# The main branch's last two tiles in an order written out by hand: last weights turned first, last statistics in front of the narrowing

## The chip, the cores and the metric

The kernel runs on one core of a Trainium2 chip. The time is what the device takes for one execution, in microseconds; the kernel before is given as the median of three runs. A core has five engines with an instruction stream each: TensorE (PE) for matrix products, VectorE (DVE), ScalarE (ACT), GpSimd (POOL) and SyncE (SP), which here issues the transfers. An engine takes its instructions in order, so an instruction that waits holds up everything behind it on its engine. TensorE writes its results to PSUM banks, from which DVE and ACT read them.

## The reference, cut to what matters

Two layers, each of which adds an attention branch multiplied by a gate branch to a stream `x` of 2 x 2048 rows of 256 numbers, in float32. The change lies in the second layer's main branch, and in its last step:

```python
x = x + ob @ w_out + b_out                                    # ob: the attention's sums
h2 = _ln(x, ln2_g, ln2_b)                                     # statistics, then scaling
m = gelu(h2 @ w1 + b1, approximate=False) @ w2 + b2           # 256 -> 1024 -> 256
s = x + m                                                     # the main branch's result
...
x = x_in + s * g                                              # g: the gate branch, x_in: the stream
```

The attention is local: a block of 64 queries sees its own and the preceding block of 64 keys, for 16 heads.

## The kernel before, in words

The 4096 rows are 32 tiles (`NT`) of 128 rows, in 8 groups (`NG`) of 4 (`GT`). The gate branch has been computed by the time of interest and lies in `G` (the profile calls its tile `stream`). The main branch is in `main_branch`. `head(g)` prepares a group's queries and keys. `attention(g)` goes over its four tiles. For tile n it has two half tiles, 2n and 2n + 1: `turn_weights` transposes the softmax weights of a half tile (8 transposes of 128x128, L1640), `small` computes the scores of the half tile two further on (`score`, L1607) and then `total`, the weighted sums of this one (L165). The four steps of `finish(n)` end a tile: `take` copies the sums out of PSUM, `divide` transposes them and divides (PE L188, DVE L192), `back` transposes back (PE L252, copy on ACT L254), and `out` multiplies with the output weights and adds the residual on DVE (PE L261, DVE L1672), which gives the tile's row of `y`. `take` stands in the tile's own slot; `divide`, `back` and `out` of tile n - 1 stand in the slot of tile n, so those of the last tile, 31, are left over for `finale`.

`forward(g, t0, nt)` is the feed-forward part of `nt` tiles of a group:

- `moments(t)`: two DVE statistics operations (L79, L80) on a tile of `y`; `ln_rsqrt`: two POOL operations (L84, L85) that give the scale.
- `norm(t)`: DVE scales the tile into `h2` (L88; the profile's `h`), then POOL adds the bias row `b2` to `y` (L1717).
- `turn(c)`: PE transposes `h2`, one half of its columns for each c (L1724), and `affine` copies it to `h2T`, on DVE for c = 0 (L1591) and on ACT for c = 1 (L1589).
- `widen`: four calls of two chunks each; a chunk is two products of 128 hidden units (PE L1741) and a GELU on ACT (L1748). `u` and `ge` hold the result.
- `again(t)`: SP loads the residual rows of a tile again (L1732, into `xs_b`).
- `narrow(t)`: eight products (PE L1754), a DVE sum with `y` (L1758), POOL's product with `G` (L1759) and sum with the residual (L1760), and the output transfer on SP (L1761).

All instructions are recorded in program order; what runs on an engine when follows from that order and the waits. The order comes from `in_turn`: every lane is a list of (weight, step) with a start and an end, each step gets the place of its weight's middle, and the steps of all lanes are sorted by place. A step `none` only takes room. In the last group, `attention(7)` shares its room with the feed-forward part of group 6 (`forward(NG - 2)`) and then with that of the first two tiles of group 7, 28 and 29 (`forward(NG - 1, 0, 2)`, called the pair below). `finale` follows: tile 31's divide, back and out spread over the first 0.6 of the feed-forward of tile 30, and then, alone, the feed-forward of tile 31.

Of the kernel before, what the change touches and what calls it, by code (L numbers as in the profile page):

```python
# [9 lines left out]
ALU = mybir.AluOpType  # L10
# [4 lines left out]
NT = B * S // P  # L15
TPB = S // P
GT = 4
GW = GT * P
NG = NT // GT
# [11 lines left out]
def kernel(ctx: ExitStack, tc: tile.TileContext, io: dict, col: dict):  # L31
    nc = tc.nc
# [57 lines left out]
    def in_turn(*lanes):  # L90

        order = []
        for i, (a, b, lane) in enumerate(lanes):
            total, at = sum(w for w, _ in lane), 0.0
            for w, do in lane:
                order.append((a + (b - a) * (at + w / 2) / total, i, len(order), do))
                at += w
        for _, _, _, do in sorted(order, key=lambda x: x[:3]):
            do()
# [187 lines left out]
    G = stream.rearrange("p (n d) -> p n d", d=D)  # L287
# [531 lines left out]
    with ExitStack() as l0_ctx:  # L819
# [349 lines left out]
        groups, values, zss, accs, scores, turns, outs, ends = {}, {}, {}, {}, {}, {}, {}, {}  # L1169
# [296 lines left out]
        for g in range(NG):  # L1466
            lanes = [(0, 1, attention(g))]
# [12 lines left out]
            if g == NG - 1:  # L1480
                first, second = first_tiles
# [15 lines left out]
    def main_branch(open_pc):  # L1497
# [20 lines left out]
        groups, values, zss, accs, scores, turns, outs, ends = {}, {}, {}, {}, {}, {}, {}, {}  # L1518
# [159 lines left out]
        def attention(g):  # L1678

            lane = []  # L1680
            none = lambda: None
            for n in range(GT * g, GT * (g + 1)):
                divide, back, out = ends[n - 1] if n else [none] * 3
                take, *ends[n] = finish(n)
                ahead = (lambda n=n: project_values(n + 1)) if n + 1 < NT else none

                def small(i):

                    if i + 2 < 2 * NT:
                        score(i + 2)  # L1690
                    total(i)

                first, second = (lambda i=i: turn_weights(i) for i in (2 * n, 2 * n + 1))
                lane += [(1, first), (1.2, none), (0.7, divide), (0.6, none)]
                lane += [(1.2, lambda n=n: small(2 * n)), (1.8, none), (0.5, back), (1, none)]
                lane += [(1, second), (2, none)]
                lane += [(1.2, lambda n=n: small(2 * n + 1)), (0.3, take), (0.8, none), (0.5, out), (0.8, none), (1, ahead), (0.6, none)]
            return lane

        def forward(g, t0=0, nt=GT):  # L1700

            d = {}
            ts = range(t0, t0 + nt)
            w = nt * P

            def moments(t):
                if t == t0:
                    d["mv"] = sb(pc, [P, GT, 2], "f_mv")
                    d["rs"] = sb(pc, [P, GT], "f_rs")
                ln_moments(pc, d["mv"], t, [groups[g]["y"][:, t, :]])  # L1710

            def norm(t):
                if t == t0:
                    d["h2"] = sb(pc, [P, GT, D], "h2", 1)
                y = groups[g]["y"][:, t, :]
                normalize(d["h2"][:, t, :], y, d["mv"], d["rs"], t)
                nc.gpsimd.tensor_tensor(y, y, b2, ALU.add)  # L1717

            def turn(c):
                if not c:  # L1720
                    d["h2T"] = sb(pe, [P, 2, GW], "h2T", 1)
                tp = bank("tp")
                for i, t in enumerate(ts):
                    nc.tensor.transpose(tp[:, i * P : (i + 1) * P], d["h2"][:, t, c * P : (c + 1) * P], ident)  # L1724
                affine(d["h2T"][:, c, 0:w], tp[:, 0:w], c, "c_ln2_g", "c_ln2_b")

            def again(t):

                if (t - t0) % 2 == 0:
                    d["rr"] = sb(pe, [P, GT, P], "xs_b", 2).rearrange("p (a b) n -> p a (b n)", a=2)  # L1730
                d["r", t] = d["rr"][:, (t - t0) % 2, :]
                nc.sync.dma_start(d["r", t], rows_r[:, g * GT + t, :])  # L1732

            def widen(cs):
                if not cs[0]:
                    u = sb(pe, [P, HC, GW], "u", 1)
                    d["m"] = [u[:, c, :] for c in range(HC)] + [sb(pe, [P, GW], "ge") for _ in range(8 - HC)]
                for c in cs:
                    mm = bank("s")[:, 0:w]
                    for k in range(2):  # L1740
                        nc.tensor.matmul(  # L1741
                            mm,
                            lhsT=cw["w1"][:, k, c * P : (c + 1) * P],
                            rhs=d["h2T"][:, k, 0:w],
                            start=(k == 0),
                            stop=(k == 1),
                        )
                    nc.scalar.activation(d["m"][c][:, 0:w], mm, AF.Gelu, bias=cc("c_b1", c))  # L1748

            def narrow(t):  # L1750
                mm = bank("s")[:, 0:D]
                i = t - t0
                for c in range(8):
                    nc.tensor.matmul(  # L1754
                        mm, lhsT=d["m"][c][:, i * P : (i + 1) * P], rhs=cw["w2"][:, c, :], start=(c == 0), stop=(c == 7)
                    )
                out = groups[g]["y"][:, t, :]
                nc.vector.tensor_tensor(out, mm, out, ALU.add)  # L1758
                nc.gpsimd.tensor_tensor(out, out, G[:, g * GT + t, :], ALU.mult)  # L1759
                nc.gpsimd.tensor_tensor(out, out, d["r", t], ALU.add)  # L1760
                nc.sync.dma_start(yout[:, g * GT + t, :], out)  # L1761

            lane = [(0.7, lambda t=t: moments(t)) for t in ts]
            lane += [(0.5, lambda: ln_rsqrt(d["rs"][:, t0 : t0 + nt], d["mv"][:, t0 : t0 + nt, :], 1e-5))]
            lane += [(1, lambda: None)]
            lane += [(0.7, lambda t=t: norm(t)) for t in ts] + [(0.3, lambda: None)]
            lane += [(0.7, lambda c=c: turn(c)) for c in range(2)] + [(0.7, lambda: None)]
            lane += [(3.4, lambda c=c: widen((c, c + 1))) for c in range(0, 8, 2)]
            lane += [(0, lambda t=t: again(t)) for t in ts]
            return lane + [(3.4, lambda t=t: narrow(t)) for t in ts]  # L1770

        def begin():
            project_values(0)
            score(0)

        lanes = []
        for g in range(NG):
            lanes.append((g, g + 1, attention(g)))
# [2 lines left out]
            if g < NG - 3:  # L1781
                lanes.append((g + 1.27, g + 2.6, forward(g)))
        lanes += [(NG - 1.73, NG - 0.6, forward(NG - 3)), (NG - 0.73, NG - 0.25, forward(NG - 2))]
        lanes.append((NG - 0.24, NG, forward(NG - 1, 0, 2)))

        def finale():
            in_turn((0, 0.6, [(1, step) for step in ends[NT - 1]]), (0, 1, forward(NG - 1, 2, 1)))
            in_turn((0, 1, forward(NG - 1, 3, 1)))

        return [(0.1, constants)] + head(0), enter, begin, lambda: score(1), lanes, finale  # L1790

    with ExitStack() as end_ctx:
# [12 lines left out]
        lanes = list(lanes_d)  # L1805
        lanes.append((end - 0.52, end, head_c))
        lanes.append((end - 0.75, end, last_but_one[:-6]))
        none = lambda: None
# [157 lines left out]
```

## Time and profile before

| | |
|---|---|
| median of 3 runs (lowest to highest) | 2928.58 us (2925.85 to 2929.3) |
| the profiled execution | 2958.06 us |
| its span, first to last instruction | 2956.2 us |
| mean granted TensorE clock over the span | 0.965 |
| PE busy in 2920 to 2930, 2930 to 2940, 2940 to 2956 us | 6.63, 5.98 and 7.37 us |
| waits of PE at L1724 for DVE's `h`, 2895 to 2957 us | 10.1 us, 4 times, longest 3.6 |
| waits of DVE at L88 for POOL's `f_rs`, same stretch | 4.4 us, 3 times, longest 2.0 |

The profile is of one execution, recorded with a tracer, and that one is slower than the timed runs; times in the trace are microseconds from its span's start. "PE busy" counts products that overlap by their modelled ends; start times are the firmer numbers. The granted clock is given as a share of full speed. A line of a time line names the start, the duration, the engine, the line in the kernel, the operation, out<-in by the program's names with partitions x elements, how many instructions were merged, and in brackets the engine's wait before it with who ended it. For products (not for transposes) a time line counts two instructions where the program has one, so a count of 16 is 8 products of the program.

### The profile page before, as it was taken

To read this page: it belongs to the slowest core of one execution; us is meant where nothing else is said; L and a number is where in the kernel's file an instruction comes from. 1 tells how busy PE (TensorE), PEld (TensorE's weight loads), DVE (VectorE), ACT (ScalarE), POOL (GpSimd) and SP (SyncE) were. 2 spreads that over 40 slices of the span, in tenths; PEclk is the share of its full clock that TensorE was granted. 3 is DMA by queue.
4 is the path that set the end of the run, shared out by engine and by line. 5 is a ranking of instruction groups with operands and counts; after the bars stand their busy time and mean duration, and the time that the engine had idled before them with its cause. 6 is when DMAs were issued, how large, how long until landed. Compare 5 with 4: busy or idle time off the path is not lost.

```text
span 2956.2 us, 72449 instructions
## 1 busy us (share of the span) xinstructions
PE 2733.7 (92%) x28246; PEld 1966.3 (67%) x28246; DVE 1881.2 (64%) x6668; ACT 1693.4 (57%) x4624; POOL 1093.2 (37%) x1255
## 2 busy tenths in 40 slices
PE   5899999999986899999999999999998999999997
PEld 3778777787764666666666666666666666666666
DVE  6566555655676777776676776767667555555542
ACT  3677767776763454444444444555543567777672
POOL 1233333333335555454544444444443112222212
PEclk9999999999988999999999999999999899999999
DMA  6122222222212100101000010000001010000000
GB/s 218 62 84 92 77 83 70 78 85 85 70 37 87 30 26 16 30 23 33 23 12 30 16 39 8 9 5 5 5 5 31 19 37 23 23 23 23 16 16 22
DMA packets 84501, 123.88 MB, mean 42 GB/s; under 512 B 7744, under 2 KB 74720, under 8 KB 79168
## 3 DMA queue, kind: packets, MB, share of 16 engines
q1 hardware_dynamic: 80752, 109.94, 11.5%
q0 software_dynamic: 3408, 9.31, 1.1%
q8 instruction: 225, 3.69, 0.5%
q14 instruction: 116, 0.95, 0.1%
HBM read 88.95 MB, written 21.89 MB: 37 GB/s over the span
## 4 chain that ended last, share of the span: by engine, by line
PE 62%; DVE 15%; ACT 13%; issue 5%; POOL 4%; DMA 1%; SPq 0%; POOLq 0%; DVEq 0%; ACTq 0%
PE s L744 10%; PE s L535 5%; PE s L766 4%; PE s L1133 4%; PE tp L151 3%; ACT pr L136 3%; PE s L663 3%; PE s L1754 3%; ACT pr L1627 3%; PE s L551 2%; PE s L1116 2%; PE s L1741 2%; PE s L458 2%; DVE pr L107 2%; PE acc L488 2%
## 5 line engine op out<-in xcount | busy, mean ns | idle before, releaser
L579 POOL TENSOR_TENSOR inv<-inv,nhalf 128x16 f32<-128x16 f32 x64 | 187.2, 2926 | 449.1 <-DVE inv L578 448.9
L478 ACT ACTIVATE pr<-pr,mn 128x192 f32<-128x192 f32 (+2 forms) x512 | 188.4, 438 | 236.3 <-DVE mn L107 216.0
L107 DVE CUSTOM_DVE_ANT_0 pr<-s,cst 128x128 f32<-128x128 f32 (+2 forms) x1024 | 261.5, 315 | 96.0 <-PE s L1607 73.8
L744 PE MATMUL s<-h2T,d_w 128*128 128x512 f32 x704 | 316.8, 603 | 0.0
L69 ACT COPY pt<-tp 128x384 f32<-128x384 f32 (+3 forms) x320 | 156.5, 495 | 234.5 <-PE tp L151 210.4
L1627 ACT ACTIVATE pr<-pr,mn 128x128 f32<-128x128 f32 x512 | 198.1, 388 | 107.4 <-DVE mn L107 107.1
L136 ACT ACTIVATE pr<-pr,mn 128x192 f32<-128x192 f32 (+2 forms) x512 | 222.9, 436 | 54.8 <-DVE mn L107 51.2
L71 DVE COPY pt<-tp 128x384 f32<-128x384 f32 (+3 forms) x320 | 181.1, 566 | 110.2 <-PE tp L151 79.9
L568 POOL TENSOR_TENSOR scr<-scr,tab 128x512 f32<-128x512 f32 x128 | 168.2, 1314 | 186.1 <-DVE scr L71 186.0
L535 PE MATMUL s<-d_wqkv,hT 128*128 128x512 f32 x512 | 236.8, 603 | 0.0
L744 PEld LDWEIGHTS s<-h2T,d_w 128*128 128x128 f32 x704 | 133.7, 194 | 152.7 <-issue 150.8
L151 PE MATMUL tp<-cst,pr 128*128 128x128 f32 x1488 | 211.9, 277 | 17.3 <-ACT pr L478 10.0
L151 PEld LDWEIGHTS tp<-cst,pr 128*128 128x128 f32 x1488 | 175.2, 143 | 54.4 <-issue 21.5
L757 DVE SCALAR_TENSOR_TENSOR u<-s,cols,ge 128x512 f32<-128x512 f32 x96 | 71.9, 749 | 203.3 <-PE s L744 122.8
L766 PE MATMUL s<-d_w,u 128*128 128x256 f32 x768 | 178.4, 382 | 0.0
L1133 PE MATMUL s<-Wo,it 128*128 128x128 f32 x1248 | 161.6, 285 | 2.4 <-DVE mnl L107 2.3
L1759 POOL TENSOR_TENSOR x<-x,stream 128x256 f32<-128x256 f32 x32 | 23.3, 728 | 373.2 <-DVE x L1758 373.2
L1133 PEld LDWEIGHTS s<-Wo,it 128*128 128x128 f32 x1248 | 152.6, 199 | 10.7 <-issue 7.1
L766 PEld LDWEIGHTS s<-d_w,u 128*128 128x128 f32 x768 | 142.8, 190 | 23.6 <-issue 3.7
L535 PEld LDWEIGHTS s<-d_wqkv,hT 128*128 128x128 f32 x512 | 94.0, 194 | 91.1 <-issue 90.8
L107 DVE CUSTOM_DVE_ANT_0 pr<-s,cst_a 128x192 f32<-128x192 f32 (+2 forms) x512 | 144.0, 347 | 14.5 <-PE s L114 13.1
L1116 PE MATMUL s<-xsT,w 128*128 128x128 f32 x1248 | 149.5, 279 | 0.2
(302 smaller groups left out, 6457.3 us busy)
## 6 DMA issues: line engine op xcount, KB each, us to landing
w<-in_W1b_dram SPq DMA_DIRECT2D x39, 1028.0 KB
ysort<-ys SPq DMA_DIRECT2D x39, 128.0 KB
xn<-in_L_attn_x_dram SPq DMA_DIRECT2D x8, 512.0 KB
rows_n<-xn SPq DMA_DIRECT2D x8, 512.0 KB
rows_s<-s SPq DMA_DIRECT2D x32, 128.0 KB
stream<-in_L_attn_x_dram SPq DMA_DIRECT2D x8, 512.0 KB
sg<-rows_s SPq DMA_DIRECT2D x8, 512.0 KB
rows_r<-stream SPq DMA_DIRECT2D x8, 512.0 KB
```

The lines of the kernel that those rows point to most:

```text
L71: nc.vector.tensor_copy(out, in_)
L107: nc.vector.tensor_tensor_reduce(pr, sc, mask, 1.0, CAP, ALU.add, ALU.min, mn)
L136: nc.scalar.activation(w, w, AF.Exp, bias=mn[:, v : v + 1], scale=-1.0, accum_out=zs[:, v, blk, s : s + 1])
L151: nc.tensor.transpose(tp[:, k * P : (k + 1) * P], pr[:, k, :, :].rearrange("p v j -> p (v j)"), ident)
L478: nc.scalar.activation(p, p, AF.Exp, bias=mn[:, w : w + 1], scale=-1.0)
L535: nc.tensor.matmul(mm, lhsT=heads[r][:, k, t * P : (t + 1) * P], rhs=wqkv_d[l][:, k, j * INNER : (j + 1) * INNER], start=(k == 0), stop=(k ...
L579: nc.gpsimd.tensor_tensor(inv.rearrange("p a h -> p (a h)"), inv.rearrange("p a h -> p (a h)"), nhalf, ALU.pow)
L744: nc.tensor.matmul(mm, lhsT=w1[l][:, k, c, :], rhs=d["h2T"][:, k, 0:w], start=(k == 0), stop=(k == 1))
L766: nc.tensor.matmul(mm[:, 0:D], lhsT=d["u"][:, c, i * P : (i + 1) * P], rhs=w2[l][:, c, :], start=(c == 0), stop=(c == HC - 1),)
L1116: nc.tensor.matmul(mm[:, c * P : (c + 1) * P], lhsT=w[:, k * FF + ic * P : k * FF + (ic + 1) * P], rhs=d["xsT"][:, k, :], start=(k == 0), ...
L1133: nc.tensor.matmul(mm, lhsT=d["it"][:, ic, :], rhs=late["Wo"][:, ic, h], start=(ic == 0), stop=(ic == FF // P - 1))
L1627: nc.scalar.activation(w, w, AF.Exp, bias=mn[:, v : v + 1], scale=-1.0, accum_out=zs[:, v, blk, st : st + 1])
```

## The change

The attention lane of tile 31 is cut: behind its second `turn_weights` stand `out` of tile 30, at once, and the first three steps of tile 30's feed-forward (load of the residual, `moments`, `ln_rsqrt`), then `small` and `take`; the room behind is shorter. The pair's lane gives its two `narrow` steps to `finale`, and keeps the room up to the end of the group, so that its other steps and those of group 6 get other places. `finale` runs a list written out by hand. For a single tile, `again` stands first in the lane; POOL's two operations become a step `gated` of their own, ahead of `narrow`, on `y` alone; and `narrow` ends in two DVE operations: the product of PE's result with `G`, and the sum with the gated `y`. For the pair and the groups before, `narrow` issues what it did.

```diff
@@ -1693,12 +1693,17 @@
                 first, second = (lambda i=i: turn_weights(i) for i in (2 * n, 2 * n + 1))
                 lane += [(1, first), (1.2, none), (0.7, divide), (0.6, none)]
                 lane += [(1.2, lambda n=n: small(2 * n)), (1.8, none), (0.5, back), (1, none)]
+                if n == NT - 1:
+                    lane += [(1, second), (0.5, none), (0.5, out), (0, last_rows[0]), (0.3, last_rows[1]), (0.3, last_rows[2]), (0.7, none)]
+                    lane += [(1.2, lambda n=n: small(2 * n + 1)), (0.3, take), (0.5, none)]
+                    continue
                 lane += [(1, second), (2, none)]
                 lane += [(1.2, lambda n=n: small(2 * n + 1)), (0.3, take), (0.8, none), (0.5, out), (0.8, none), (1, ahead), (0.6, none)]
             return lane
 
         def forward(g, t0=0, nt=GT):
 
+            single = nt == 1
             d = {}
             ts = range(t0, t0 + nt)
             w = nt * P
@@ -1730,6 +1735,12 @@
                     d["rr"] = sb(pe, [P, GT, P], "xs_b", 2).rearrange("p (a b) n -> p a (b n)", a=2)
                 d["r", t] = d["rr"][:, (t - t0) % 2, :]
                 nc.sync.dma_start(d["r", t], rows_r[:, g * GT + t, :])
+
+            def gated(t):
+
+                out = groups[g]["y"][:, t, :]
+                nc.gpsimd.tensor_tensor(out, out, G[:, g * GT + t, :], ALU.mult)
+                nc.gpsimd.tensor_tensor(out, out, d["r", t], ALU.add)
 
             def widen(cs):
                 if not cs[0]:
@@ -1755,9 +1766,13 @@
                         mm, lhsT=d["m"][c][:, i * P : (i + 1) * P], rhs=cw["w2"][:, c, :], start=(c == 0), stop=(c == 7)
                     )
                 out = groups[g]["y"][:, t, :]
-                nc.vector.tensor_tensor(out, mm, out, ALU.add)
-                nc.gpsimd.tensor_tensor(out, out, G[:, g * GT + t, :], ALU.mult)
-                nc.gpsimd.tensor_tensor(out, out, d["r", t], ALU.add)
+                if single:
+                    x = groups[g]["x"][:, t, :]
+                    nc.vector.tensor_tensor(x, mm, G[:, g * GT + t, :], ALU.mult)
+                    nc.vector.tensor_tensor(out, x, out, ALU.add)
+                else:
+                    nc.vector.tensor_tensor(out, mm, out, ALU.add)
+                    gated(t)
                 nc.sync.dma_start(yout[:, g * GT + t, :], out)
 
             lane = [(0.7, lambda t=t: moments(t)) for t in ts]
@@ -1766,13 +1781,19 @@
             lane += [(0.7, lambda t=t: norm(t)) for t in ts] + [(0.3, lambda: None)]
             lane += [(0.7, lambda c=c: turn(c)) for c in range(2)] + [(0.7, lambda: None)]
             lane += [(3.4, lambda c=c: widen((c, c + 1))) for c in range(0, 8, 2)]
-            lane += [(0, lambda t=t: again(t)) for t in ts]
+            if single:
+                lane.insert(0, (0, lambda: again(t0)))
+                lane.append((1, lambda: gated(t0)))
+            else:
+                lane += [(0, lambda t=t: again(t)) for t in ts]
             return lane + [(3.4, lambda t=t: narrow(t)) for t in ts]
 
         def begin():
             project_values(0)
             score(0)
 
+        pair, before_last, alone = forward(NG - 1, 0, 2), forward(NG - 1, 2, 1), forward(NG - 1, 3, 1)
+        last_rows = [f for _, f in before_last]
         lanes = []
         for g in range(NG):
             lanes.append((g, g + 1, attention(g)))
@@ -1781,11 +1802,18 @@
             if g < NG - 3:
                 lanes.append((g + 1.27, g + 2.6, forward(g)))
         lanes += [(NG - 1.73, NG - 0.6, forward(NG - 3)), (NG - 0.73, NG - 0.25, forward(NG - 2))]
-        lanes.append((NG - 0.24, NG, forward(NG - 1, 0, 2)))
+        lanes.append((NG - 0.24, NG, pair[:-2]))
 
         def finale():
-            in_turn((0, 0.6, [(1, step) for step in ends[NT - 1]]), (0, 1, forward(NG - 1, 2, 1)))
-            in_turn((0, 1, forward(NG - 1, 3, 1)))
+
+            divide, back, out = ends[NT - 1]
+            (_, first), (_, second) = pair[-2:]
+            (_, _, _, _, norm_b, _, turn_b, turn_b2, _, *widen_b, gated_b, narrow_b) = last_rows
+            (rows_c, mom_c, scale_c, _, norm_c, _, turn_c, turn_c2, _, *widen_c, gated_c, narrow_c) = [f for _, f in alone]
+            order = [first, norm_b, divide, turn_b, turn_b2, second, rows_c, back, widen_b[0], out, mom_c, scale_c]
+            order += [*widen_b[1:], gated_b, norm_c, turn_c, turn_c2, narrow_b, *widen_c, gated_c, narrow_c]
+            for step in order:
+                step()
 
         return [(0.1, constants)] + head(0), enter, begin, lambda: score(1), lanes, finale
```

## The prediction

> **What bounds the kernel now.** I read the page first, then the chain that ended last, then the time lines of PE, DVE and POOL for the last 100 us, the granted clock in slices of 1 us, and last the instruction order of both built programs.
>
> ```profile
> PE 2733.7 (92%) x28246; PEld 1966.3 (67%) x28246; DVE 1881.2 (64%) x6668; ACT 1693.4 (57%) x4624; POOL 1093.2 (37%) x1255
> PE   5899999999986899999999999999998999999997
> ```
>
> PE bounds the kernel as a whole; only the last slice, 74 us long, falls to 7 tenths. The diff touches the main branch's last two groups, so that slice is where it can act. The built programs are equal on PE up to about 2842 us, and from there to 2896 us the time line has only 0.8 us of pauses on PE, near 2855, at a turning that the diff leaves where it is. Reordering inside that stretch keeps the set of instructions, so I take the transposes of turn_weights(62) to start at 2895.36 in both. After them PE waits at three places, always at L1724, the turning of the normalized rows `h`:
>
> ```profile
> 2895.36 1.09 PE L1640 MATMUL tp<-cst,pr 128*128 128x128 f32 x8
> 2896.29 0.60 PE L188 MATMUL tp<-cst,aT 128*128 128x128 f32 x4
> 2899.39 0.33 PE L1724 MATMUL tp<-cst,h 128*128 128x128 f32 x1 [2.50 <-DVE h L88]
> 2900.60 0.90 PE L1724 MATMUL tp<-cst,h 128*128 128x128 f32 x3 [0.89 <-DVE h L88]
> ...
> 2919.89 0.60 PE L188 MATMUL tp<-cst,aT 128*128 128x128 f32 x4
> 2923.61 0.44 PE L1724 MATMUL tp<-cst,h 128*128 128x128 f32 x2 [3.12 <-DVE h L88]
> ...
> 2937.84 0.44 PE L1724 MATMUL tp<-cst,h 128*128 128x128 f32 x2 [3.56 <-DVE h L88]
> 2938.75 5.17 PE L1741 MATMUL s<-h2T,d_w 128*128 128x128 f32 x32 [0.47 <-DVE h2T L1591]
> ```
>
> (Columns: start, duration, instructions, wait before them and who ended it. Starts, not the overlapping durations, are used below.) Each wait is one chain: DVE statistics (L79, L80), POOL power (L84, L85), DVE scaling (L88). The clock follows each wait with a delay:
>
> ```profile
> 2938.00:2939.00 1.00, 0.53 (x3) 0.58 0.00 0
> 2939.00:2940.00 1.00, 1.00 (x6) 0.50 0.02 8
> 2940.00:2941.00 1.00, 1.00 (x6) 0.50 0.06 16
> 2941.00:2942.00 1.00, 1.00 (x9) 0.71 0.00 0
> 2942.00:2943.00 1.00, 1.00 (x12) 1.00 0.00 0
> ```
>
> (Slice, its length, PE busy and count, granted clock.) About 4 us after PE went idle the clock halves for some 3.3 us, at 2900.8, 2924.7 and 2938.4: PE has work again by then and pays. At the end DVE adds the narrowing's sum (L1758), POOL does two operations (L1759, L1760), and the output goes out:
>
> ```profile
> 2947.48 0.42 DVE L1758 TENSOR_TENSOR x<-s,x 128x256 f32<-128x256 f32 x1 [8.79 <-PE s L1754]
> 2947.98 0.72 POOL L1759 TENSOR_TENSOR x<-x,stream 128x256 f32<-128x256 f32 x1 [9.39 <-DVE x L1758]
> 2948.78 0.72 POOL L1760 TENSOR_TENSOR x<-x,xs_b 128x256 f32<-128x256 f32 x1
> ```
>
> **The change, part by part.** PE prices at full clock, by starts: a narrowing 3.55 us (2912.02 to 2915.57); two widening chunks of a pair 1.73 (2905.27 to 2907.00); four chunks of a single tile 1.79 (2928.88 to 2930.67), so 0.45 each; `out` 0.87; `total` 0.60; turn_weights 0.87; four divide transposes 0.44; `back` 0.22; two turnings 0.28.
>
> *First turning (tiles 28, 29).* Group 6's last narrowing now stands ahead of out(29), and the moments directly behind it. DVE reads out(29) at 2894.47, as values(30) keeps its PE start of 2894.28. Then tile 28's statistics, the values' sum at 2895.46, and tile 29's statistics, ending at 2896.43. POOL takes 0.09 + 0.27 + 0.71 (first chain: L84 at 2897.91, L85 at 2898.18), so `h` starts on DVE at 2897.53 instead of 2898.92, and its second tile 0.33 later, no longer behind the two divide operations. A turning starts 0.47 after its L88: PE idles from 2896.45 to 2898.0 and 0.2 more, against 3.39 before. Then two turnings, divide, two turnings and total; the widening starts at 2899.8 (its second input is ACT's, ready near 2899.95) and two chunks end at 2901.5, not 2905.05. **Gain 3.5**: 1.65 of waiting and 1.8 of half clock (turnings 0.5, total 0.44, two chunks 2.58 against 1.73).
>
> *Second turning (tile 30).* out(30) is now before total(63), three widening blocks in; its moments and POOL's rsqrt end near 2909.1, beside widening and narrowing on PE. PE goes on 0.22 + 1.73 + 0.87 + 1.74 + 0.87 + 0.60 + 1.74 + 3.55, to 2912.85, and 0.44 for divide. The new wait: `h` of tile 30 stands on DVE behind the first narrowing's sum (PE's result at 2913.0), so it starts at 2913.31 and the turning at 2913.78. Behind it on DVE stand only divide and the h2T copy, both needed after the next narrowing. PE idles about 0.35, against 3.12. The 0.25 before the widening goes, since the pair's second narrowing (2914.06 to 2917.6) covers the h2T copies; so does the half clock, 3.50 against 1.79 for four chunks. **Gain 2.8 + 0.25 + 1.7 = 4.75.**
>
> *Third turning (tile 31).* back at 2917.6, two chunks, out(31) at 2918.73, DVE at 2919.79, statistics to 2920.76. POOL has finished the pair's last two operations at 2919.8, so L84 and L85 run to 2921.7; `h`, and the turning could start at 2922.18. PE is in tile 30's six other chunks until 2922.28. Nothing is left to wait for, by 0.1 us; if that cover is gone, each us of lateness is a us of PE. Tile 30's narrowing (to 2926.1) covers tile 31's h2T copies. **Gain 3.6 of wait, 0.65 between turning and widening, 1.4 of half clock (5.0 against 3.58 for eight chunks): 5.65.**
>
> *End.* POOL's two operations of tiles 30 and 31 run ahead: tile 31's residual load is issued on SP behind the pair's second output near 2920.3, must land before POOL's last operation near 2924.8, and DVE needs that at 2933.9. Loads of this size here occupy the DMA until about 2 us after issue; slack suffices. What follows PE's last result is two DVE operations. The new pair has no row: the nearest are L1758 (0.42) and the step from a DVE operation to one that needs its result (L79 to L80, 0.45). So 0.9 against 2.05 from L1758's start to L1760's end: **gain 1.1**, bounded by 0.7 (a second operation as slow as POOL's) and 1.2 (0.34, the step of unrelated DVE operations). Other ACT, SP and bank waits end under PE work; the residual loads have over 10 us, and widening chunks go at 0.45 on PE and 0.43 on ACT.
>
> Sum: 3.5 + 4.75 + 5.65 + 1.1 = **15.0 us**. The profiled execution took 2958.06 (span 2956.2), so it becomes 2943.1. The three runs' median is 29.5 lower; I keep the difference: **2913.6**.
>
> **Where a row decides the clock.** What stays is a first gap of 1.55 plus 0.2. Gaps of 2.4 to 3.6 in the trace are followed by the half clock without exception. The nearest below are five gaps of 1.89 at L188 in this same branch (2472, 2543, 2614, 2686, 2757): two of five were followed by it; of the ten between 1.2 and 1.75 that stand alone after 240 us, one (1.53 at 425). I take full clock. A drop costs at most half of 3.3 us: 1.65.
>
> The Trainium skill, "TensorE: Matmul & The Clock Gate", section "What's actually happening", says the gate closes after an idle window of about 3.4 us that runs freely; by it alone a 1.6 us gap never closes it and the sum stays 15.0, but the two of five gaps above contradict it when taken alone. Section "Part 4: PE-mode transpose" of that page says transposes do not count as a busy PE; then the quiet stretch would run from 2895.36 to total's start near 2899.1, 3.7 us, and the sum would be the first rival's 13.35.
>
> **Rivals.** (1) *The first gap still halves the clock*, 4 us later, in the pair's widening: for it the two of five, and the transposes on both sides of the gap; against it the shorter gap. 15.0 − 1.65: **2915.2**. (2) *The third chain is late*: the 0.1 us of cover fails, since DVE, POOL and PE all stand in line for it. At worst its wait and clock return (3.56 + 1.4): **2918.6**; against it, PE must be ahead by as much as before. (3) *The waits return at both later turnings* because each chain stands behind another tile's result on DVE and POOL: 3.5 + 1.1 stay and 0.5 of the rest: **2923.5**, no difference. The instruction order speaks against it: only one foreign DVE operation stands ahead of either `h`. (4) *Slower*: the first gap halves the clock and it does not lift, since PE's stream is cut up by turnings. A half clock of length L costs L/2, so the gain is gone at L = 30 us, and slower by 0.2% needs 42 us, most of the finale. At 50 us: −15.0 + 25, **2938.6**. The longest half clock with PE mostly busy is 10.5 us (2334 to 2344), and all three of the last slice lifted after 3.3. The Trainium skill, same page, "Seeing it yourself", tells of a clock stuck low for over 50 us; no run here shows it. (5) *It doesn't do what it says* is out: the built order has the steps where the list puts them.
>
> **How the numbers follow.** Forecast 0.52; (1) 0.30; (2) 0.10; (3) 0.05; (4) 0.03. This kernel's measurement tells about 0.2%, 5.9 us, from no change: faster is below 2922.7. So faster 0.92, same 0.05, slower 0.03. Range: all remaining waits gone would be 2.1 below the forecast, 2911.5, and the lowest run lay 2.7 below its median: 2908.8. At the top, (2) at its worst, 2918.6, with the highest run's 0.7 and something for the tail: 2920. Cases 1 to 2 lie inside.
>
> **What would show it.** Right: PE's wait at the first turning near 1.6, at the second under 0.7, none at the third; clock full after 2905; from the last narrowing's end to the output's issue about 1 us. Wrong: a wait above 1 us at the second or third turning with DVE or POOL behind it; a pause in PE before 2895 (then the equal start was false); a half clock in a stretch without a gap; DVE's last operation waiting for POOL.

## The result, and the profile after

| | before | after |
|---|---|---|
| median (lowest to highest), 4 runs each | 2928.77 us (2925.85 to 2929.3) | 2907.23 us (2902.99 to 2909.59) |
| ratio after to before, 95% interval | | 0.9918 (0.9906 to 0.993) |
| the profiled execution, its span | 2958.06, 2956.2 us | 2909.59, 2907.8 us |
| start of the transposes of turn_weights(62), end of the span | 2895.36, 2956.2: 60.84 us | 2865.11, 2907.8: 42.69 us |
| mean granted TensorE clock | 0.965 | 0.972 |

The kernel became faster, as forecast, but by more: 2907.23 us is 6.4 below the forecast of 2913.6 and 1.6 below the low end of its range. The spans of the two profiles differ by 48.4 us, and most of that is not the change: 30.25 us are there when turn_weights(62) starts, and 30.00 of them at the last scores ahead of the first reordered step (2840.13 us before, 2810.13 after), up to where both programs issue the same. The 0.25 between the two points is the change's: the profiles take 55.23 and 55.24 us from those scores to turn_weights(62) before, 54.98 to 55.00 in three profiles after. From turn_weights(62) on, called **the stretch** below, the change is worth 60.84 - 42.69 = **18.15 us**; the prediction had 15.0.

The page of the profile after: the line of busy times, and PE in the forty slices.

```profile
PE 2703.4 (93%) x28246; PEld 1950.4 (67%) x28246; DVE 1882.8 (65%) x6670; ACT 1694.0 (58%) x4624; POOL 1094.6 (38%) x1255
PE   5899999999987899999999999999998899999999
```

PE's last slice, 7 tenths before, now reads 9. The time line of PE after, from turn_weights(62) on (start, duration, what, and in brackets the wait before it):

```profile
2865.11 1.09 PE L1640 MATMUL tp<-cst,pr 128*128 128x128 f32 x8
2867.86 0.56 PE L1729 MATMUL tp<-cst,h 128*128 128x128 f32 x2 [1.66 <-DVE h L88]
...
2883.90 0.44 PE L1729 MATMUL tp<-cst,h 128*128 128x128 f32 x2 [0.47 <-DVE h L88]
...
2889.61 2.84 PE L1752 MATMUL s<-h2T,d_w 128*128 128x128 f32 x24
2892.83 0.41 PE L1729 MATMUL tp<-cst,h 128*128 128x128 f32 x2 [0.38 <-DVE h L88]
...
2896.53 3.73 PE L1752 MATMUL s<-h2T,d_w 128*128 128x128 f32 x32
```

The turning is L1729 here (L1724 before), the widening L1752, the narrowing L1765. Of the waits for `h` 1.66, 0.47 and 0.38 us are left, where 3.39, 3.12 and 3.56 stood, and eight widening chunks of tile 31 take 3.73 instead of 5.17: the clock is full in every slice of the stretch. The close, DVE's time line after:

```profile
2903.76 0.42 DVE L1771 TENSOR_TENSOR x<-s,stream 128x256 f32<-128x256 f32 x1 [6.07 <-PE s L1765]
2904.28 0.43 DVE L1772 TENSOR_TENSOR x<-x,x 128x256 f32<-128x256 f32 x1
```

and the issue of the last output on SP, after and then before:

```profile
2904.74 0.33 SPq L1776 DMA_DIRECT2D out_dram<-x  x1
```

```profile
2949.53 0.33 SPq L1761 DMA_DIRECT2D out_dram<-x  x1
```

From DVE's first operation on PE's last result to this issue it is 0.98 us, 2.05 before: the 1.1 of the prediction. But from the issue to the end of the span it is 3.06 us, and **6.67 before**: the same transfer of one tile, and 3.61 us less behind it. What lay there is told by SP's waits at the very end, before and after (us in total, times, longest; PEq is PE's instruction queue, and the line is the program's last):

```profile
SPq L1962 <- PEq L1962: 4.3, 2, 3.8
SPq L1962 <- DMA out_dram<-x: 1.3, 1, 1.3
```

```profile
SPq L1990 <- DMA out_dram<-x: 1.3, 1, 1.3
SPq L1990 <- PEq L1990: 0.7, 2, 0.5
```

The wait for the output transfer is 1.3 in both. A second wait of 3.8 us, in which SP waits for the other engines to arrive, is 0.5 after. PE's last product had ended at 2947.4, 8.8 us ahead of the end of the span; who was late is seen in the instructions of the program's last line. Each engine's queue has instructions called DRAIN there; these are POOL's, before and after (duration in ns min/median/max, first and last start):

```profile
L1962 POOLq DRAIN  x3: 45/107/6645, 2948.7 to 2955.9; - x3
```

```profile
L1990 POOLq DRAIN  x3: 45/107/6652, 2894.9 to 2907.5; - x3
```

One drain of POOL lasts 6.65 us; the longest of another engine lasts 2.99, on PE's queue from 2944.4. Before, POOL's starts at 2948.7, as its last sum starts (L1760, done at 2949.50), and is over at 2955.4, 0.8 ahead of the end of the span. After, it starts at 2894.9, with POOL's last sum, and is over at 2901.5, while PE still narrows.

### The profile page after: what moved, and what is told of

Its sections match the earlier page's. It is cut to its first block, busy times and chain, and to the rows that moved or that the text cites. A ratio compares the mean times of both kernels' runs of the same rounds, so it can differ in the third digit from the quotient of the medians.

```text
span 2907.8 us, 72452 instructions
## 1 busy us (share of the span) xinstructions
PE 2703.4 (93%) x28246; PEld 1950.4 (67%) x28246; DVE 1882.8 (65%) x6670; ACT 1694.0 (58%) x4624; POOL 1094.6 (38%) x1255
## 4 chain that ended last, share of the span: by engine, by line
PE 64%; DVE 15%; ACT 13%; POOL 3%; issue 3%; DMA 1%; SPq 0%; DVEq 0%; POOLq 0%; ACTq 0%
PE s L744 10%; PE s L535 5%; PE s L766 5%; PE s L1133 4%; PE s L1765 3%; PE tp L151 3%; ACT pr L136 3%; PE s L1752 3%; PE s L663 3%; PE s L551 3%; PE s L1116 2%; ACT pr L1627 2%; PE s L458 2%; DVE pr L107 2%; PE acc L488 2%
## 5 line engine op out<-in xcount | busy, mean ns | idle before, releaser
L744 PE MATMUL s<-h2T,d_w 128*128 128x512 f32 x704 | 310.7, 593 | 0.0
```

What stands on the lines that cost most here:

```text
L744: nc.tensor.matmul(mm, lhsT=w1[l][:, k, c, :], rhs=d["h2T"][:, k, 0:w], start=(k == 0), stop=(k == 1))
```

## The experiments

Two theories stood at the start. **A**: the 3.6 us at the close are POOL's drain, which ends 5.9 us after POOL's last operation wherever that stands; the change took it off the end by moving POOL's two operations ahead. **B**: the close is shorter for another reason (less work in the chain behind PE, another state of queues), or the surplus lies in PE's stream. Later runs priced the turnings one by one. The stretch is the measure throughout: it repeats to 0.2 us between executions of one kernel (save for one case, told below), while their timed runs scatter by some 20 us. The timed runs are named where they were taken.

**Both kernels once more.** Without edits, beside the others.

> The kernel before, unchanged, with a profile of its own. The profiled execution that the prediction was worked out from took 2958.06 us, 29 more than the median of the timed ones, and differed from the profile of the changed kernel by 28 us before the last slice, where the programs are equal. Theory A (that execution drew more half clocks in the gate branch, 1030 to 1440 us, and the finale is the same in every execution): this one takes about 2929, reaches the last group some 28 us earlier, and its stretch from the transposes of turn_weights(62) to the span's end is again 60.8 us (within 2). Theory B (the profiler itself costs some 29 us): this one too takes about 2958.

> The changed kernel, unchanged, once more. Theory A (the finale is the same in every execution): 42.7 us from the transposes of turn_weights(62) to the end, within 2; time 2903 to 2910. Theory B (the 18 us that the last slice gained is a lucky draw of the clock at the first turning): a half clock after the 1.66 us gap, 44.4 us.

Before: stretch 61.04 us (60.84 in the first profile), drain 6.647 us, ratio 1.0001 (0.9985 to 1.0017). After: stretch 42.71 (42.69), ratio 0.9945 (0.9926 to 0.9965), medians 2946.88 and 2927.37. So the stretch repeats, and the times do not: neither 2929 nor 2958 came for before (profiled execution 2946.66, median of the runs beside it 2946.54), and the changed kernel lies above its 2903 to 2910. The kernel before has medians of 2929.58 to 2949.25 us in the four later comparisons, each on another chip.

**The tail alone.** The kernel before, with tile 31's POOL operations ahead of its narrowing and two DVE operations behind it; no step of PE is moved.

```diff
@@ before: narrow, and the lane of tile 31 @@
-                nc.vector.tensor_tensor(out, mm, out, ALU.add)
-                nc.gpsimd.tensor_tensor(out, out, G[:, g * GT + t, :], ALU.mult)
-                nc.gpsimd.tensor_tensor(out, out, d["r", t], ALU.add)
+                if g * GT + t == NT - 1:
+                    x = groups[g]["x"][:, t, :]
+                    nc.vector.tensor_tensor(x, mm, G[:, g * GT + t, :], ALU.mult)
+                    nc.vector.tensor_tensor(out, x, out, ALU.add)
+                else:
...
+                lane += [(0, lambda: gated(t0))]
```

> The kernel before with one part of the change: for tile 31 alone, POOL's product with G and sum with the residual run ahead of the narrowing, and two DVE operations follow it. Order untouched. Theory A (the span of before ends with POOL's drain, 6.65 us after POOL's last operation): end 4.7 us earlier than before, from DVE's first operation to the span's end 4.0 us instead of 8.7. Theory B (as the prediction had it, the close after the last operation is the output transfer's and stays): 1.1 us earlier, 7.6 us from DVE's first operation to the end.

The stretch is 56.07 us, 4.97 less than the 61.04 of before on the same chip. DVE's first operation of the tail, in the time line of this run, whose span ends at 2942.7:

```profile
2938.63 0.42 DVE L1766 TENSOR_TENSOR x<-s,stream 128x256 f32<-128x256 f32 x1 [8.71 <-PE s L1760]
```

It is 4.07 us from there to the end, 8.72 before and 4.04 after. So the whole surplus of the close comes with the tail, with PE's order untouched. Timed, the ratio is 0.9993 (0.998 to 1.0005): 4.97 us of 2947 would be 0.9983, which the interval holds, as it holds no gain.

**Only POOL's last operation late again.** The changed kernel, and a copy of 128 numbers on POOL behind tile 31's last DVE operation. Nobody reads it; the output does not wait for it.

```diff
@@ after: narrow, tile 31 (second run: tile 30) @@
                     nc.vector.tensor_tensor(out, x, out, ALU.add)
+                    if g * GT + t == NT - 1:
+                        nc.gpsimd.tensor_copy(sb(pc, [P, 1], "last", 1), out[:, 0:1])
```

> The changed kernel with one more POOL operation, a copy of 128x1 that reads tile 31's finished rows and is used by nobody. Theory A (drain of POOL): the span ends about 4.6 us later than the changed kernel's, 6.65 us and the closing semaphores after the small copy. Theory B (the output transfer closes the span): no change, since the copy of about 0.2 us lies beside a transfer of 2.

> The changed kernel with the small POOL copy reading tile 30's finished rows instead of tile 31's: 7 us before the last result. Theory A (the drain starts with POOL's last operation and lasts 5.9 us behind it): no change at the end, 42.7 us from turn_weights(62), since 5.9 us are over before the output's transfer closes. Theory B (any further POOL operation near the end costs): 43 or more.

With the copy at tile 31 the stretch is 46.59 us, 3.90 longer than 42.69. POOL's time line, and POOL's queue in the program's last line:

```profile
2921.97 0.19 POOL L1774 COPY last<-x 128x1 f32<-128x1 f32 x1 [9.15 <-DVE x L1772]
```

```profile
L1992 POOLq DRAIN  x3: 45/107/6097, 2921.9 to 2928.6; - x3
```

The copy ends at 2922.16 and the drain at 2928.0, 5.8 us later, with 0.9 to the end of the span. SP's wait for the others is back at 4.0 us. The 4.6 us that were expected were too many: behind the copy the drain takes 6.10 us and not 6.65. With the same copy at tile 30 the stretch is 42.72, no difference:

```profile
L1992 POOLq DRAIN  x3: 45/107/6650, 2920.6 to 2929.5; - x3
```

There the copy holds up tile 31's product and sum behind it on POOL. The last of them ends at 2921.39, 8.4 us ahead of the end of the span (12.2 in the changed kernel), and the drain is over at 2927.3. An operation of 0.19 us thus costs 3.9 or nothing by its place: theory A.

**The order alone.** The changed kernel, whose last tile keeps the old tail (a DVE sum, then two POOL operations).

```diff
@@ after: narrow, and finale's list @@
+                    if g * GT + t == NT - 1:
+                        nc.vector.tensor_tensor(out, mm, out, ALU.add)
+                        gated(t)
+                    else:
...
-            order += [*widen_b[1:], gated_b, norm_c, turn_c, turn_c2, narrow_b, *widen_c, gated_c, narrow_c]
+            order += [*widen_b[1:], gated_b, norm_c, turn_c, turn_c2, narrow_b, *widen_c, narrow_c]
```

> The changed kernel, but tile 31 ends as before: one DVE sum, then POOL's two operations. All of the order stays. Theory A (POOL's drain, 5.9 us after its last operation's end, closes the span, and the parts add up): 47.4 us from the transposes of turn_weights(62) to the end, 4.7 more than the changed kernel's 42.7, PE's part equal to its to 0.2 us. Theory B (only the two operations cost): 43.8.

The stretch is 47.48, so the order alone is worth 60.84 - 47.48 = 13.4 us and the tail on top of it 47.48 - 42.69 = 4.8. That these two make 18.15 is only arithmetic; that the parts do not depend on each other is seen from the tail alone, which gave 4.97 with the old order. Timed, 0.9952 (0.9935 to 0.9968).

**Each later turning without its cover.** In the first run tile 30's out goes back behind the pair's first narrowing and its moments behind the second, in the second run tile 31's moments, scaling and turning go back behind tile 30's narrowing.

```diff
@@ after: lane of tile 31 and finale's list, first run @@
-                    lane += [(1, second), (0.5, none), (0.5, out), (0, last_rows[0]), (0.3, last_rows[1]), (0.3, last_rows[2]), (0.7, none)]
+                    lane += [(1, second), (0.5, none), (0, last_rows[0]), (1.8, none)]
...
-            order = [first, norm_b, divide, turn_b, turn_b2, second, rows_c, back, widen_b[0], out, mom_c, scale_c]
+            order = [first, out_b, second, mom_b, scale_b, divide, norm_b, turn_b, turn_b2, rows_c, back, widen_b[0], out, mom_c, scale_c]
@@ after: finale's list, second run @@
-            order = [first, norm_b, divide, turn_b, turn_b2, second, rows_c, back, widen_b[0], out, mom_c, scale_c]
-            order += [*widen_b[1:], gated_b, norm_c, turn_c, turn_c2, narrow_b, *widen_c, gated_c, narrow_c]
+            order = [first, norm_b, divide, turn_b, turn_b2, second, rows_c, back, widen_b[0], out]
+            order += [*widen_b[1:], gated_b, narrow_b, mom_c, scale_c, norm_c, turn_c, turn_c2, *widen_c, gated_c, narrow_c]
```

> The changed kernel with the second turning put back: out(30) and tile 30's statistics behind the pair's first narrowing, the statistics, divide and turning behind the second, as before. Theory A (this turning is worth what the prediction summed for it, wait and half clock): PE waits 3.1 us at tile 30's turning and 0.25 at its widening, the clock halves some 4 us after the wait's start, 4.4 us more than the changed kernel from turn_weights(62) to the end (47.1). Theory B (the half clock is drawn by the first turning and not by this wait): 2.9 us more, clock full.

> The changed kernel with the third turning put back: tile 31's statistics, norm and turning behind tile 30's narrowing, as before; the residual's load and the early POOL operations stay. Theory A (wait and half clock as summed): PE waits 2.4 to 3.6 us at the turning (3.56 before, less up to 1.2 for the POOL operations that no longer stand in front) and 0.47 at the widening; 4.0 to 5.2 us more than the changed kernel (46.7 to 47.9). Theory B (no half clock, because PE was busy without a pause for long before): 2.6 to 3.8 more.

The stretches are 47.25 and 47.68 us, 4.56 and 4.99 above 42.69. The time lines of PE of the two runs:

```profile
2886.73 0.44 PE L1730 MATMUL tp<-cst,h 128*128 128x128 f32 x2 [3.12 <-DVE h L88]
2887.01 0.38 PE L252 MATMUL tp<-cst,o 128*128 128x128 f32 x2
2887.64 1.67 PE L1753 MATMUL s<-h2T,d_w 128*128 128x128 f32 x8 [0.25 <-DVE h2T L1591]
```

```profile
2901.39 0.44 PE L1729 MATMUL tp<-cst,h 128*128 128x128 f32 x2 [2.98 <-DVE h L88]
2902.30 5.46 PE L1752 MATMUL s<-h2T,d_w 128*128 128x128 f32 x32 [0.47 <-DVE h2T L1591]
```

Both waits come back with the half clock behind them: two chunks in 1.46 us by starts (0.89 after), eight with modelled end in 5.46 (3.73 after). In the second run the wait is 2.98 and not 3.56: POOL's operations of tile 30 are out of the chain's way (L84 starts 0.09 us behind the statistics, 1.13 before), and DVE's second operation of tile 30, which is new there, takes about 0.5 of that back.

**More work, less time.** The kernel before, with three products of 128x512 that nobody reads put into the second gap and three into the third. No step is moved.

```diff
@@ before: forward, a single tile @@
+            def fill():
+                mm = bank("s")
+                for i in range(3):
+                    nc.tensor.matmul(mm, lhsT=cw["w1"][:, 0, 0:P], rhs=cw["w1"][:, 1, 0:512], start=(i == 0), stop=(i == 2))
...
+            if nt == 1:
+                lane += [(0, fill)]
             lane += [(0.7, lambda c=c: turn(c)) for c in range(2)] + [(0.7, lambda: None)]
```

> The kernel before with three products of 128x512 that nobody reads, in front of the turning of tile 30 and again in front of tile 31's: PE works through most of each wait, and the turnings start when they did. Theory A (half of what a wait costs comes after it, as half clock): the waits shrink to under 1.6 us, the clock stays full after 2905, and from turn_weights(62) to the end it takes 57.8 to 58.4 instead of 61.0, faster by up to 3.2 us with more work. Theory B (the half clock costs nothing that counts, DVE and POOL set the pace): 61.0.

The stretch is 57.89 us, 2.95 less than 60.84. PE's time line around the third turning:

```profile
2900.69 2.74 PE L1738 MATMUL s<-d_w 128*128 128x512 f32 x6
2904.42 0.44 PE L1724 MATMUL tp<-cst,h 128*128 128x128 f32 x2 [0.99 <-DVE h L88]
2905.32 3.84 PE L1749 MATMUL s<-h2T,d_w 128*128 128x128 f32 x32 [0.47 <-DVE h2T L1591]
```

The chain is as late as before, but PE waits 0.99 instead of 3.56, the clock stays full, and the eight chunks take 3.84 instead of 5.17. This is the price of the half clock by itself, at both turnings 1.7 + 1.4 = 3.1 in the prediction.

**The third turning's 0.38 us.** POOL's two operations of tile 30 stand behind tile 31's normalising, not ahead of it.

```diff
@@ after: finale's list @@
-            order += [*widen_b[1:], gated_b, norm_c, turn_c, turn_c2, narrow_b, *widen_c, gated_c, narrow_c]
+            order += [*widen_b[1:], norm_c, gated_b, turn_c, turn_c2, narrow_b, *widen_c, gated_c, narrow_c]
```

> The changed kernel with one swap in its last lane: POOL's two additions of tile 30 (the rows' half and the product's half of the gated residual) are issued behind tile 31's normalising step instead of ahead of it, so that no two-input operation of POOL runs while DVE normalises tile 31. Measured so far: DVE's normalising step at the third turning takes 0.81 us in every profile of the changed order where POOL's addition lies beside it, 0.41 us where none does, and PE waits 0.38 us at that turning, where the prediction had none. Theory A (the addition beside it doubles the step): the step takes 0.41 us, the wait at the third turning falls to between 0 and 0.1 us, and from the first transpose of the main branch's last pair to the end of the span it is 42.3 us instead of 42.7. POOL's last operation moves back by under 2 us and still ends more than 8 us ahead of the close, so its end is hidden as before. Theory B (the chain of moments, reciprocal root and normalising is simply longer than the cover there): the step takes 0.41 or 0.81, the wait stays at 0.38 us and the stretch at 42.7 us.

The stretch is 42.33 us, 0.36 less. First DVE and then POOL in the changed kernel, then DVE and PE in this run:

```profile
2891.87 0.81 DVE L88 TENSOR_SCALAR h<-x,f_mv,f_rs 128x256 f32<-128x256 f32 x1 [0.96 <-POOL f_rs L85]
```

```profile
2891.80 0.73 POOL L1742 TENSOR_TENSOR x<-x,stream 128x256 f32<-128x256 f32 x1
```

```profile
2905.43 0.41 DVE L88 TENSOR_SCALAR h<-x,f_mv,f_rs 128x256 f32<-128x256 f32 x1 [0.96 <-POOL f_rs L85]
```

```profile
2905.99 0.41 PE L1729 MATMUL tp<-cst,h 128*128 128x128 f32 x2
```

The same operation takes 0.81 us when POOL's product (two inputs) has begun 0.07 ahead of it, and 0.41 when POOL is idle; without the 0.40 the turning follows its widening with no wait.

**A version of my own.** The first turning gets cover too: out of tile 29 is issued earlier, the pair's lane begins earlier, so that its statistics stand ahead of group 6's last narrowing; tile 30's scaling stands ahead of the pair's first narrowing. The second run adds the swap above.

```diff
@@ after: attention, lanes, finale's list @@
+                if n == NT - 2:
+                    lane += [(1, second), (0.5, none), (0.5, out), (1, none)]
+                    lane += [(1.2, lambda n=n: small(2 * n + 1)), (0.3, take), (1.6, none), (1, ahead), (0.6, none)]
+                    continue
...
-        lanes.append((NG - 0.24, NG, pair[:-2]))
+        lanes.append((NG - 0.30, NG, pair[:-2]))
...
-            order = [first, norm_b, divide, turn_b, turn_b2, second, rows_c, back, widen_b[0], out, mom_c, scale_c]
+            order = [norm_b, first, divide, turn_b, turn_b2, second, rows_c, back, widen_b[0], out, mom_c, scale_c]
```

> A version of my own, from the changed kernel: out(29) one place earlier, the pair's lane starting at 0.30 instead of 0.24 before the end, so that tiles 28's and 29's statistics stand ahead of group 6's last narrowing, and tile 30's norm ahead of the pair's first narrowing's sum. Theory A (the waits left, 1.66 + 0.2 at the first turning and 0.47 at the second, go, and nothing new is late): from score(63), 49.6 us before the changed kernel's end, to the end 47.2 to 47.6; in time 2 us of 2907, under what the measurement tells. Theory B (the softmax minimum operations that now stand behind the statistics on DVE are late and PE waits for the scores instead): 49 to 51.

> The version of my own (the first turning given cover too: the output sums of tile 30 ahead of the second half of its neighbour's products, and the pair's lane begun a little earlier) with the swap of POOL's additions added. From the start of the scores of the last group to the end of the span the changed kernel took 49.53 us and the version without the swap 47.19 us. Theory A: 46.8 us, with a wait of at most 0.1 us at the third turning. Theory B: 47.2 us with the wait of 0.38 us kept. Against the kernel before: ratio 0.991 to 0.994, not to be told from the changed kernel by the timed runs, whose difference scatters by 3 us, while the stretch itself repeats to 0.1 us.

Here turn_weights(62) has another place, so the measure runs from the scores of half tile 63 to the end: 49.53 us in the changed kernel, 47.19 in the first run and 46.79 in the second. Of the first turning's 1.66 a wait of 0.56 + 0.41 is left, at the second and (second run) at the third none. What is left at the first turning has the third's mark: in the first run the pair's two scalings on DVE take 1.40 us together beside POOL's product and sum, and 0.73 in the changed kernel. No run here takes it away. Timed against before: 0.9943 (0.992 to 0.9965) and 0.9931 (0.9908 to 0.9954); the changed kernel, repeated beside the first, has 0.994 (0.9919 to 0.9961). The 2.3 to 2.7 us are seen in the profiles; the timed runs do not tell them from none.

**The changed kernel a third time**, in that same comparison.

> The changed kernel again, beside that version on one chip: 42.7 us from turn_weights(62) to the end, 18 us (14 to 22) faster than before by the timed runs.

This profile is the exception: a stretch of 44.40 us, 1.7 longer. The first gap is 1.66 as always, but the half clock follows it, as PE's time line shows:

```profile
2892.65 0.56 PE L1729 MATMUL tp<-cst,h 128*128 128x128 f32 x2 [1.66 <-DVE h L88]
...
2893.80 1.02 PE L165 MATMUL acc<-pt,v 64*32 64x128 f32 x32
2894.75 3.28 PE L1752 MATMUL s<-h2T,d_w 128*128 128x256 f32 x8
```

The values' sums take 1.02 (0.67 in the first profile) and two chunks 3.28 (1.99); the granted clock is 0.50 from 2894 to 2897 and full after 2898. This is rival (1), at 44.40 - 42.69 = 1.71 against its 1.65; by the slices the half clock lasts 3.42 us, and half of that is 1.71. Nine profiles have this gap of about 1.66 with the same instructions around it (three of the changed kernel and those of the edits that leave the first turning alone); one shows the half clock.

## Why the prediction was wrong in its size, point by point

**First turning, 3.5: right.** From turn_weights(62) to the end of two widening chunks it is 6.33 us, 9.69 before: 3.36. The wait left is 1.66 (the sum had 1.55, and 0.2 more).

**Second turning, 4.75: right.** 0.47 us of wait are left (0.35 in the sum), 0.25 ahead of the widening and the half clock are gone. Taken back alone it costs 4.56.

**Third turning, 5.65: 0.38 too much.** "Nothing is left to wait for, by 0.1 us" did not hold, by rival (2)'s mechanism at under a tenth of its worst price: the cover went because DVE's normalising (the scaling, L88) ran beside POOL's product and took 0.81 us. The sum priced it as 0.41, from rows in which POOL was idle beside it (2937.37 before). The swap of the two shows it. The Trainium skill's "GPSIMD Engine Reference", section "1. Specifications", says that GpSimd shares its SBUF interfaces with VectorE and contends with those DVE instructions that run in a 2-port mode or have two SBUF inputs. The trace does not tell whether the scaling is one of them; it does show the two in each other's way, by 0.40 us of one operation. Taken back alone, this turning costs 4.99.

**PE's part together**: 13.9 predicted; from turn_weights(62) to DVE's first operation on the last result it was 52.12 and is 38.65, so 13.47.

**End, 1.1: the step that failed.** It measured 8.72 - 4.04 = **4.68 us**. The prediction priced "what follows PE's last result" as engine operations up to the output's issue (right: 2.05 to 0.98), and carried all that lies behind the issue over unchanged. Its bounds of 0.7 and 1.2 were bounds of two DVE operations, not of the close, so the range could not hold what the close would do. The missing 3.6 us were in the profile of before: the 3.8 us that SP waits in the program's last line, and the drain of 6.645 us on POOL's queue, which the time line of POOL does not list among its operations. The tail alone, the late copy and the copy at tile 30 show that it is POOL's last operation, by its place and not its work, that decides.

**The sum**: 15.0 - 0.4 (PE) + 3.6 (close) = 18.2, the measured 18.15. With it the forecast would have been 2928.58 - 18.15 = 2910.4 us, inside the range.

**The other 3.2 us**, from 2910.4 to 2907.23: 0.25 of them are the change's, where the prediction took turn_weights(62) to start at the same time in both programs. The rest is not the change as far as the profiles tell. The gain of the first comparison, 20.5 to 27.5 us by its interval, does not hold 18.15; the two later ones, 0.9945 (0.9926 to 0.9965) and 0.994 (0.9919 to 0.9961) of some 2948 us, give 10 to 22 and 12 to 24 us, and do. What scatters lies ahead of the stretch: turn_weights(62) starts at 2865.11, 2891.59 and 2889.90 us in three profiles of the changed kernel, and at 2895.36 and 2883.86 in two of before. An example of where: the time lines of PE before and after, at the same place of both programs.

```profile
1240.71 1.07 PE L488 MATMUL acc<-v,pt 64*64 64x65 f32 x36
...
1242.68 0.35 PE L488 MATMUL acc<-v,pt 64*64 64x65 f32 x3 [0.43 <-issue]
...
1246.02 8.30 PE L744 MATMUL s<-h2T,d_w 128*128 128x512 f32 x16
```

```profile
1227.73 1.20 PE L488 MATMUL acc<-v,pt 64*64 64x65 f32 x48
...
1229.35 7.03 PE L744 MATMUL s<-h2T,d_w 128*128 128x512 f32 x16
```

In the profile before, PE pauses five times among these products with nothing that the profile shows to wait for ("issue"), and the half clock follows (0.50 from 1246 to 1248); the passage takes 13.4 us against 8.5. What makes PE pause there in one execution and not in another is open: no run here was made for it. The step "I keep the difference" of 29.5 us between profile and median carried a difference whose cause stays open; the scatter was allowed 2.7 us at the low end, and three runs showed too little of it.

**The rivals.** (1) is real, with its price, in one of nine profiles; it had 0.30. If the transposes on both sides of that wait are counted as quiet too, the quiet lasts 3.90 us (2865.11 to 2869.01) in all nine alike, so that neither length alone says when the clock drops. (3), (4) did not happen: no half clock in the stretch lasted over 4 us in any profile while PE had work. The prediction's three half clocks of before start, by the slices, at 2900.6, 2924.5 and 2938.2 and last 3.4 us each; its figures are 0.2 late and 0.1 short, which changes no term by more than 0.1. (5) is out. The chance of 0.92 for faster was justified; the range was too narrow at its low end, by the close and by the scatter.

## What to carry to other kernels

The end of a program is priced by everything that closes the span, not by the last engine operation: look up what every queue does in the program's last line, and which one arrives last. Here work on POOL costs nothing extra if its last operation ends some 3.6 us ahead of the last output's issue (estimated from the rows: 5.9 us of drain and 0.8 to the end, against 3.06 from issue to end; the nearest run, the copy at tile 30, has 5.3), and up to about 4 us if it comes last (3.90 for the late copy). When a chain is to fit into a cover of a few tenths, price each of its operations with the neighbour that the new order puts beside it on the other engine.

## What the runs showed of the hardware that was not expected

POOL's drain at the program's end is over 5.8 to 5.9 us after the end of POOL's last operation, behind a sum of 128x256 and behind a copy of 128x1 alike. In the five profiles that end with a POOL operation the span ends 6.70 to 6.75 us after it; in the ten others that operation ends 8.4 us or more ahead of the end, and the span ends 4.03 to 4.11 us after the start of DVE's first operation on the last result. What POOL does in these 5.9 us no run here shows.

DVE's normalising and POOL's product of 128x256 lengthen each other; at two places of the changed kernel where they meet, the one that starts second is the longer one. At the third turning POOL starts 0.07 us ahead, and DVE takes 0.81 instead of 0.41; at the second (2883.44 and 2883.60 in the changed kernel) DVE starts ahead and keeps its 0.40, and POOL takes 0.83 instead of 0.73; only the first has a run that takes the neighbour away. Whether DVE runs at half its rate or stands until POOL is done, these rows do not tell.

A pause of 1.66 us is followed by the half clock in one of nine profiles of the same instructions. The Trainium skill, "TensorE: Matmul & The Clock Gate", section "What's actually happening", has the gate close after an idle window of about 3.4 us that runs freely; the one case speaks against a window of that length taken by idle time alone, and the eight others against counting on the drop.
